# A list schedule for a four-layer graph network on one Trainium2 core: the bound on small matmuls applied in every state, and separate offsets for the second group of a pair

## The chip, the cores and the metric

The kernel runs on one core of one Trainium2 chip. The metric is the device time of one execution in microseconds (us). Before the change it is 2170.12 us, the median of three runs (2168.34 to 2181.28).

## The reference

128 graphs of 64 nodes with 512 features each go through four layers; everything is fp32. After each layer `x = layernorm(x + layer(x))`.

```python
# layer 0: attention from one vector; y = x @ w, s = y @ a
A = exp(leaky(tanh((s_i + s_j) / 8) * 8)) * adj;  A = A / rowsum(A) * rowsum(adj)
out = A @ x @ w
# layer 1: weight = adj * exp((x Wq^T)(x Wk^T)^T), normalised over rows, times x Wv^T
# layer 2: w_i = <q_i, (adj @ (k * mask))_i> * mask / sqrt(512);  out = softmax(w) * (x @ Wv)
# layer 3: two hypergraph convolutions with H = (adj != 0)
h = layer_norm(relu(D^-1 H B^-1 H^T (x @ W1^T) + b1)) * gamma + beta      # 512 -> 1024
out = D^-1 H B^-1 H^T (h @ W2^T) + b2 + x                                 # 1024 -> 512
```

## The kernel before, in words

**Tiling.** Tokens are cut into 64 tiles of 128 (two graphs each). A group is two tiles (256 tokens), so there are 32 groups; a pair is two groups, so there are 16 pairs. One group's work is cut into 16 steps: attention of layer 0 (steps 0 to 2), layer 1 (3 to 6), layer 2 (7 to 11), layer 3 (12 to 15). Steps 0 to 12 are recorded for each group by `run(g)`. Steps 12 to 15 of layer 3 are recorded by `run_rest(n)` for both groups of a pair together, except in the first and the last pair (`APART_3A`), where each group goes alone; there its first product has 512 output columns.

**Two kinds of matmul.** The dense products use the whole 128x128 array ("whole"); they are written as fast matrix products (seven products for eight blocks, forty-nine for sixty-four), with weights streamed from DRAM through eight `ring` buffers. The products with a graph's 64x64 matrices use quarters of the array (mode "quarters": 64 rows, 64 columns, four at a time) and the layer's scores use halves (mode "columns"); both are "divided". `gathered` makes two divided operations of 16 matmuls, so 32 for each 512-feature side; `scores` makes two operations of 8. For the 1024-feature side of layer 3, step 14 of one group needs two `gathered`, that is 64 divided matmuls, and a pair needs 128. `over_graph` has mode "any": one matmul of 128 rows when it is put among whole ones, two of 64 rows when it is put among divided ones. Every fp32 matmul is two passes in the trace, each with its weight load; a transpose is one.

**The order.** The kernel records all operations first, each with an engine, a cost estimate, what it reads and writes, and a key. `Order.run` is a list scheduler: on each engine the ready operation with the smallest key goes next, if its buffers are free. The result is only an order for each engine: the chip executes it in that order and waits on semaphores, and a pause that the scheduler reckoned with is not in the program. The key is `BASE[g]` plus a place in the 16 steps (from how much work still follows the operation) minus an offset: `order.early`, taken from `EARLY[step]`. `PREPARED` places the preparation of weights in the first pairs.

**The choice on TensorE.** All ready TensorE operations go to `Order.choose`. A switch between whole and divided is reckoned with `TURN` 145. While the mode is "whole", a divided operation is taken if it is due earlier than the whole one by more than `NEAR` (by more than 0 where 48 divided matmuls are ready). While the mode is divided, another divided operation is taken only if it is due no later than `FAR` behind the first whole one, and if the last 64 matmuls that end with it take at least 3500 (`BLOCK, REST = 64, 3500`, in ns of the scheduler's reckoning):

```python
        if first[0][0] < 0 or first[0][2].mode == "any" or not (whole and divided):
            return first
        if mode == "whole":
            ...
        fits = [f for f in divided if f[0][0] <= whole[0][0][0] + self.FAR
                and now + f[0][2].cost >= began[f[0][2].matmuls - self.BLOCK] + self.REST]
```

So this bound holds in one state only: the mode is divided and a whole operation is ready as well. With no whole operation ready, with the first operation of negative key, or on the way from whole to divided, it is not asked.

**Buffers.** Eight PSUM banks (`bank`), eight `ring` buffers for weights, 14 of `k4`, two of `h`. `product` is a count, not memory: so many dense products may be under way at once, each with two banks for its running sums and more for single products.

All instructions that the scheduler orders carry line 1459 in the profile (the call in `pinned`), so they are told apart by the names of their tiles: `kept,h` is the gather of step 14, `kept,x` that of step 12, `e,x` that of step 1, `k,k` the scores, `k,e` the attention times values, `e,same` the `over_graph`, `bh,kept` and `ones,adj` the preparation of a chunk of adjacency; `ring,k`, `ring,h` and `k,m` are the dense products, `ident,x` the transposes.

## Time and profile before

| what | value |
|---|---|
| median of three runs | 2170.12 us |
| the profiled execution | 2169.41 us |
| its span (first to last instruction) | 2167.3 us |
| granted TensorE clock, mean | 0.993 |
| TensorE matmul busy | 2118.1 us, 98% of the span |
| VectorE, ScalarE, GpSimd busy | 1489.6, 1205.9, 455.2 us |
| passes on TensorE | 21467 |
| DMA | 422.36 MB, 195 GB/s mean |
| distance from one pair to the next, mid-kernel | 132.0 us |

The profiled execution is 0.7 us under the median, and its span 2.1 us under its own time. The profile page gives busy time by engine, the span in 40 slices, and the costliest groups; the answers to "what did this engine wait for" and the timeline name an idle stretch and what ended it. "issue" as the thing waited for means that no semaphore, DMA or engine in the profile ended the wait. A pass's shown duration is longer than the distance to the next pass, because passes overlap; what a pass costs is read from the distance between starts.

### The profile page before, as it was taken

To read this page: it belongs to the slowest core of one execution; us is meant where nothing else is said; L and a number is where in the kernel's file an instruction comes from. 1 tells how busy PE (TensorE), PEld (TensorE's weight loads), DVE (VectorE), ACT (ScalarE), POOL (GpSimd) and SP (SyncE) were. 2 spreads that over 40 slices of the span, in tenths; PEclk is the share of its full clock that TensorE was granted. 3 is DMA by queue.
4 is the path that set the end of the run, shared out by engine and by line. 5 is a ranking of instruction groups with operands and counts; after the bars stand their busy time and mean duration, and the time that the engine had idled before them with its cause. 6 is when DMAs were issued, how large, how long until landed. Compare 5 with 4: busy or idle time off the path is not lost.

```text
span 2167.3 us, 54072 instructions
## 1 busy us (share of the span) xinstructions
PE 2118.1 (98%) x21467; PEld 1839.7 (85%) x21467; DVE 1489.6 (69%) x4346; ACT 1205.9 (56%) x2698; POOL 455.2 (21%) x434
## 2 busy tenths in 40 slices
PE   8999999999999999999999999999999999999998
PEld 4898788888888888888888888888888988888885
DVE  5766776685766858667686676867667686675854
ACT  2554855564555646466464565645556456564645
POOL 1210421212212112121221202122121121202211
PEclk9999999999999999999999999999999999999999
DMA  8887875554646546465563655536464464545545
GB/s 283 279 279 270 308 245 185 193 186 150 218 140 210 180 168 206 135 203 177 183 220 110 212 183 188 193 127 226 145 215 165 162 216 145 192 159 189 185 171 193
DMA packets 166315, 422.36 MB, mean 195 GB/s; under 512 B 34928, under 2 KB 52528, under 8 KB 166064
## 3 DMA queue, kind: packets, MB, share of 16 engines
q1 hardware_dynamic: 166064, 418.92, 56.3%
q8 instruction: 169, 2.77, 0.5%
q14 instruction: 82, 0.67, 0.1%
HBM read 382.77 MB, written 36.08 MB: 193 GB/s over the span
## 4 chain that ended last, share of the span: by engine, by line
PE 95%; issue 1%; DMA 1%; DVE 1%; ACT 1%; SPq 0%; POOLq 0%; DVEq 0%; ACTq 0%
PE bank L1459 95%; ACT k L1459 1%; DVE k L1459 1%; DMA k<-in_wk_dram 0%; DMA adj<-mask_rows 0%; SPq L1459 0%; DMA ring<-w 0%; DMA adj<-in_adjT_dram 0%; DVE h L1459 0%; ACT e L1459 0%; ACT h L1459 0%; DVE x L1459 0%; DVE col L1459 0%; DVE ring L1459 0%; ACT m L1459 0%
## 5 line engine op out<-in xcount | busy, mean ns | idle before, releaser
L1459 PE MATMUL bank<-ring,k 128*128 128x256 f32 x4940 | 1178.3, 388 | 5.7 <-ACT k L1459 4.1
L1459 PEld LDWEIGHTS bank<-ring,k 128*128 128x128 f32 x4940 | 909.0, 191 | 154.4 <-issue 23.5
L1459 ACT COPY k<-bank 128x512 f32<-128x512 f32 (+1 forms) x934 | 429.2, 484 | 485.0 <-PE bank L1459 378.6
L1459 DVE SCALAR_TENSOR_TENSOR x<-bank,col,x 128x256 f32<-128x256 f32 (+1 forms) x832 | 402.1, 502 | 242.8 <-PE bank L1459 231.4
L1459 PEld LDWEIGHTS bank<-k,m 128*128 128x128 f32 x3584 | 434.2, 192 | 13.3 <-DVE col L1459 1.3
L1459 PE MATMUL bank<-k,m 128*128 128x128 f32 x3584 | 441.4, 276 | 0.3 <-DVE col L1459 0.3
L1459 DVE TENSOR_TENSOR k<-bank,k 128x256 f32<-128x256 f32 (+1 forms) x678 | 296.7, 459 | 182.5 <-PE bank L1459 140.1
L1459 POOL TENSOR_TENSOR col<-col,mhalf 128x2 f32<-128x2 f32 (+1 forms) x161 | 111.1, 693 | 880.4 <-DVE col L1459 509.4
L1459 ACT ACTIVATE k<-x,col 128x512 f32<-128x512 f32 x256 | 184.2, 722 | 189.9 <-DVE col L1459 188.9
L1459 PE MATMUL bank<-ring,h 128*128 128x256 f32 x1024 | 233.1, 381 | 0.0
L1459 ACT ACTIVATE x<-x,col,col 128x512 f32<-128x512 f32 x256 | 199.9, 812 | 59.3 <-DVE col L1459 59.2
L1459 PEld LDWEIGHTS bank<-ring,h 128*128 128x128 f32 x1024 | 193.2, 190 | 27.0 <-issue 1.5
L1459 DVE TENSOR_TENSOR k<-k 128x256 f32<-128x256 f32 (+1 forms) x349 | 145.5, 432 | 47.0 <-ACT k L1459 45.8
L1459 DVE TENSOR_TENSOR k<-k,k 128x256 f32<-128x256 f32 (+3 forms) x361 | 176.6, 493 | 0.5
L1459 POOL TENSOR_TENSOR k<-k,b3b_b 128x512 f32<-128x512 f32 x64 | 80.7, 1272 | 320.6 <-DVE k L1459 289.9
L1459 POOL TENSOR_TENSOR x<-x,bv_b 128x512 f32<-128x512 f32 x64 | 81.3, 1274 | 272.9 <-PE bank L1459 233.0
L1459 PEld LDWEIGHTS bank<-k,k 128*64 128x64 f32 (+1 forms) x2112 | 77.5, 140 | 38.6 <-issue 20.1
L1459 PE MATMUL bank<-k,k 128*64 128x64 f32 (+1 forms) x2112 | 104.8, 238 | 5.3 <-DMA k<-in_wk_dram 4.8
L1459 PEld LDWEIGHTS bank<-kept,h 64*64 64x64 f32 x4096 | 72.7, 140 | 37.9 <-issue 34.0
L1459 ACT ACTIVATE k<-bank,u_c 128x128 f32<-128x128 f32 x256 | 81.8, 364 | 41.2 <-PE bank L1459 34.3
L1459 PE MATMUL bank<-kept,h 64*64 64x64 f32 x4096 | 78.4, 226 | 24.8 <-issue 24.8
L1459 DVE TENSOR_SCALAR col<-col 128x2 f32<-128x2 f32 (+2 forms) x402 | 72.6, 190 | 40.1 <-ACT k L1459 33.9
(102 smaller groups left out, 1677.9 us busy)
## 6 DMA issues: line engine op xcount, KB each, us to landing
ring<-3a SPq DMA_DIRECT2D x196, 512.0 KB, 4.8
ring<-v SPq DMA_DIRECT2D x189, 512.0 KB, 4.2
ring<-3b SPq DMA_DIRECT2D x126, 512.0 KB, 4.8
ring<-w SPq DMA_DIRECT2D x93, 512.0 KB, 4.2
x<-in_x_dram SPq DMA_DIRECT2D x32, 512.0 KB, 6.2
ring<-v SPq DMA_DIRECT2D x63, 256.0 KB, 4.9
out_dram<-x SPq DMA_DIRECT2D x31, 512.0 KB, 6.7
ring<-w SPq DMA_DIRECT2D x31, 256.0 KB, 3.8
```

The lines of the kernel that those rows point to most:

```text
L1459: made = f(*args, **kwargs)
```

## The change

Four edits.

1. In `choose` the 3500 bound filters the divided operations at the top, so in every state. If divided operations are ready, none is allowed and no whole or "any" operation is ready, `choose` returns nothing and the scheduler asks again 100 ns later (in its own reckoning; the order of the program holds no pause).
2. `product` goes from 2 to 3.
3. The second group's and the first group's parts of steps 13 and 14 get different offsets: `LEAD`, times the number of groups that follow in the pair, so the first group of a pair gets 0.325 and -0.58 on top, the second nothing.
4. The numbers `BASE`, `PREPARED`, `FAR` and two entries of `EARLY` are set anew. The distance between pairs in `BASE` stays 8.3 (4.5 + 3.8 before, 4.6 + 3.7 after).

No operation is added to or taken from the recorded list; only the order changes, and with it how many `over_graph` are one whole or two divided matmuls.

```diff
-PREPARED = [-1.85, 7.399, 8.218, 15.311, 12.896, -0.62]
+LEAD = [0.325, -0.58]
+PREPARED = [-5.214, 7.399, 8.218, 12.615, 11.711, -0.62]
...
-    NEAR, FAR = 0.5, 4.0
+    NEAR = 0.5
+    FAR = 5.712
     ENOUGH = 48
 
-    EARLY = [2.22, 0.44, 0.0, 0.0, 0.0, -0.394, 0.0, 1.328, 0.0, 0.57, -0.17, -0.03, -0.766, -0.36, -1.408, -0.35]
+    EARLY = [2.22, 0.626, 0.0, 0.0, 0.0, -0.394, 0.0, 1.328, 0.0, 0.456, -0.17, -0.03, -0.766, -0.36, -1.408, -0.964]
...
         divided = sorted(found.get("quarters", []) + found.get("columns", []), key=lambda f: f[0][:2])
+        allowed = [f for f in divided if now + f[0][2].cost >= began[f[0][2].matmuls - self.BLOCK] + self.REST]
+        if divided and not allowed and not (whole or either):
+            return None
+        divided = allowed
         first = min((f[0] for f in (whole, divided, either) if f), key=lambda f: f[0][:2])
...
-        fits = [f for f in divided if f[0][0] <= whole[0][0][0] + self.FAR
-                and now + f[0][2].cost >= began[f[0][2].matmuls - self.BLOCK] + self.REST]
+        fits = [f for f in divided if f[0][0] <= whole[0][0][0] + self.FAR]
...
-                        found, takes = self.choose(found_pe, mode, now, began)
-                        skipped.remove(found)
+                        chosen = self.choose(found_pe, mode, now, began)
+                        if chosen is None:
+                            n += 1
+                            heappush(events, (now + 100, n, None, None))
+                        else:
+                            found, takes = chosen
+                            skipped.remove(found)
...
-    kinds["product"] = [None] * 2
+    kinds["product"] = [None] * 3
...
         for r, (g, xt, _, in_g, own, dc, dh) in enumerate(pair):
             step(13)
+            order.early += LEAD[0] * (n - 1 - r)
...
             step(14)
+            order.early += LEAD[1] * (n - 1 - r)
```

## The prediction, made before the changed kernel ran

> **What bounds the kernel now.** I read the page first (busy time, the 40 slices), then what TensorE waited for, then the timeline of one such wait, then the granted clock there.

> ```profile
> PE 2118.1 (98%) x21467; PEld 1839.7 (85%) x21467; DVE 1489.6 (69%) x4346; ACT 1205.9 (56%) x2698; POOL 455.2 (21%) x434
> ...
> q8 instruction: 169, 2.77, 0.5%
> ```

> TensorE is the bound; VectorE and ScalarE have a third and more of the span free. The queue named "instruction" moved 169 packets of 16 KB. Matmuls and weight loads are 2 x 21467 = 42934 instructions, 254 for each packet: this queue carries TensorE's own program, about 64 matmuls of two passes for each packet.

> ```profile
> PE bank L1459 <- issue: 25.9, 14, 2.8
> PE bank L1459 <- DMA k<-in_wk_dram: 4.8, 2, 4.2
> PE bank L1459 <- ACT e L1459: 4.5, 3, 3.7
> PE bank L1459 <- ACT k L1459: 4.1, 5, 1.6
> ```

> Columns: waited for; us in total, times, longest. Over half of TensorE's waiting was for nothing that the profile shows. The timeline of the worst one (start, us, instruction):

> ```profile
> 604.98 1.15 PE L1459 MATMUL bank<-k,k 128*64 128x64 f32 x32
> 606.06 1.63 PE L1459 MATMUL bank<-kept,h 64*64 64x64 f32 x96
> 607.62 0.38 PE L1459 MATMUL bank<-row_of,e 128*128 128x2 f32 x2
> 607.93 1.09 PE L1459 MATMUL bank<-k,e 64*64 64x512 f32 x8
> 608.84 0.87 PE L1459 MATMUL bank<-kept,h 64*64 64x64 f32 x44
> 612.54 1.46 PE L1459 MATMUL bank<-kept,h 64*64 64x64 f32 x51 [2.82 <-issue]
> ```

> Before the gap 182 passes, nearly all divided, ran in 4.7 us: 364 instructions, more than a packet. An instruction packet began to move 0.3 us after the gap opened and took 1.07 us; the passes went on 1.4 us after it had landed. TensorE had run out of program. The waits return every 132 us from 347 to 1667, once a pair, eleven times, always in the divided matmuls of step 14. They also slow what follows:

> ```profile
> core 0: us, PE busy (x) PEld busy (x) DVE busy (x) ACT busy (x) POOL busy (x), PEclk, DMA share, GB/s
> 345.00:357.00 12.00, 9.77 (x249) 8.91 (x249) 7.82 (x22) 7.91 (x20) 0.69 (x1) 0.86 0.35 132
> 480.00:492.00 12.00, 10.72 (x162) 9.57 (x153) 9.06 (x29) 8.85 (x23) 1.38 (x2) 1.00 0.13 42
> 609.00:621.00 12.00, 9.09 (x219) 8.34 (x208) 6.64 (x19) 8.02 (x22) 0.61 (x1) 0.86 0.11 42
> 1005.00:1017.00 12.00, 9.79 (x212) 8.92 (x205) 7.30 (x22) 7.78 (x22) 0.98 (x2) 0.86 0.07 26
> ```

> PEclk 0.86 over 12 us is 3.4 us at half clock; five of the eleven stretches have it.

> [...]

> **The price of a stall.** Take the spacing from each pass to the next in the trace, by kind: 216 ns behind a whole pass of 256 columns, 112 behind one of 128, 429 of 512, 109 behind a transpose, 15 to 16 between quarter passes, 30 between score passes. Summed over the order of all 21467 passes that is 2089 us; from the first to the last start the trace has 2155.4. So 66 us are waiting: in the eleven stretches 4.1, 1.8, 4.9, 1.5, 2.9, 4.1, 3.7, 4.1, 1.7, 3.7 and 4.9, in all 37.4; in the first 65 us 10.9; in the last 50 us 1.9; the rest in crumbs of under 0.5. The stalls cost 37.4, not 25.9, because of the slower passes behind them (in the one shown, 4.9 against a gap of 2.82).

> **The change, part by part.** It shows in the compiled order, which I compared.

> *Bound in every state: -37.4 us.* Divided runs without a whole matmul between them were up to 114 matmuls, nine of them of 102; now nearly all have 56 at most, and the one of 118 mixes gathers with the slower scores (its quickest 128 passes take 3.0 us). What counts is a block: the quickest 128 successive passes in the spacings above. Before: 1.9 us in nine pairs and 2.0 to 2.2 in three more places that are over 150 passes wide; eleven of these twelve stalled. Places of 3.1 to 4.3 us, ten of them, show no gap over 0.5 us; three narrow ones of 2.23 us (17 to 86 passes) near the end show no issue wait. After: 4.07 us in nine pairs, 3.0, 3.3 and 3.5 at three other places, and 2.23 (17 wide) once at the end. All that stalled is gone, all that is left is like what did not stall. In the stretch of step 14 the order now has 48 `kept,h`, then 8 whole matmuls (16 x 216 = 3.5 us), then 48, and so on. Bounds: a gain of 37.4 if no fetch is late, of about 25 if every pair keeps 1 us; nothing if the packet needs over 4 us.

> *More switches: +3 to +6 us.* 250 switches instead of 230. Into divided a pass costs 309 instead of 216 ns, out of it 149 instead of 15: 227 ns for a round trip, x 10 = 2.3 us. Twenty `over_graph` become whole: 2 x 112 instead of 4 x about 38 ns, 20 x 0.07 = 1.4 us; together 3.7. The spacings summed over the whole new order (21427 passes) give 2095.8, that is +6.4, with 43 neighbours that the trace lacks priced by the nearest kind. I take 5.

> *Third product, offsets, BASE: 0, from -3 to +8.* They add no instruction. What could go wrong is a wait on a bank, on evacuation, or on weights. A `ring` buffer's time from its last reader (or the load ahead of it in SP's queue, where later) to the first use of its new weights, along TensorE's spacings, was 3.1 us at worst in every middle pair before and is 4.8 after; loads land in 4.2 to 4.8 us and TensorE waited 0.3 us for them in all. So cover grows in the middle. In the first 330 us, where the queues are fullest (275 GB/s, DMA share 0.79), fifteen loads have 4.4 to 8 us, thirteen before. The work that hides evacuation is the whole products between divided runs; each uncovered one costs a ScalarE copy, 0.48 us. VectorE and ScalarE do the same list, and stand at 69% and 56%.

> *Start and end: +2.* The first 132 matmuls keep their order, so the 3.7 us wait for `ACT e` at 47 us stays, with its spell of half clock. At the end the second group's gather now stands among the first group's last products, which hides a wait of 0.9 us, but the first group's gather comes straight behind the wide product without the 1.6 us pause and the 32 `kept,x` that went ahead of it, so the copy behind it is uncovered: 0.6 before, about 2.5 after.

> Sum, from the profiled execution: 2169.4 - 37.4 + 5 + 2 = 2139.0. The median was 0.7 above that execution: 2139.7, rounded to 2140.

> **Rivals.**

> 1. *The fetch stays late.* The bound counts matmuls over a time, the packet comes when it comes. If a packet takes 4.5 us from request to use, each of the nine windows of 4.07 us and the three narrower ones still stall by about 0.5 to 1.5 us, and some bring half clock on top: +10 to +15, so 2150 to 2155. For it: the packet in the shown gap began to move only after the gap opened. Against it: ten places of 3.1 to 4.3 us without a gap.
> 2. *The first pairs lose.* Weight preparation is moved (`PREPARED`), so in SP's queue reloads of layer 0 and 2 weights now stand ahead of and among its stores; if three or four of the fifteen tight loads land 2 to 3 us late, +8 to +10: 2148 to 2150.
> 3. *Slower: a bank wait in every pair.* Three products under way hold six of eight banks; gathers need two, transposes one. If a divided run then waits for a bank at its start, TensorE stands still for copy and handoff, about 0.6 us (0.48 and the semaphore). The gain is 37.4 - 7 = 30 us, 1.9 for each of 16 pairs; so from three or four such waits in every pair there is no gain, and slower by 1% (52 us lost, 3.2 a pair) takes five to six. Against it: waits for `ACT k` were 4.1 us in the whole kernel before, five in number, and the scheduler starts an operation only when its banks are free.
> 4. *It does nothing.* Excluded: the runs of 102 are gone from the program.

> **How the numbers follow.** Forecast 0.74, own range 2133 to 2147; rival 1 0.13 (2147 to 2156); rival 2 0.08; rival 3 0.05 (over 2165). One per cent of the median, about what a measurement can tell from no change, puts the line at 2148.4. Faster by over 1%: the forecast and a little under half of rivals 1 and 2, 0.82. Within 1%: the rest of these two and a part of rival 3, 0.14. Slower: 0.04. The range for 8 in 10 leaves out rival 3, the worst of rival 1 and the best tail of the forecast (no crumbs left, no cost of switches): 2132 to 2156.

> **What would show it.** Right: issue waits of TensorE from 25.9 to under 3 us; no window of half clock between 60 and 2100 us and a mean clock of 0.995 or more; 128 to 130 us from pair to pair instead of 132; 21427 passes. Wrong in the first part: issue gaps in the stretches with `kept,h`, about one at each run. Wrong in the third: rows of TensorE waiting for `ACT k`, `DVE k` or `DMA ring` of over 10 us in all, and in which window they lie tells rival 2 (under 350 us) from rival 3 (each pair).

## The result and the profile after

The changed kernel takes 2160.87 us, the median of seven runs (2158.28 to 2165.27), against 2170.12 (2162.81 to 2181.28, seven runs) for the kernel before: ratio 0.9955, 95% interval 0.9931 to 0.9979. It is faster by half a per cent, which is less than the one per cent that the prediction took as its line, and 21 us over the forecast. The profiled execution took 2158.28 us, its span is 2156.5 us (before 2169.41 and 2167.3), its mean clock 0.997 (before 0.993).

The page after, engine row and instruction queue:

```profile
PE 2118.2 (98%) x21427; PEld 1833.8 (85%) x21427; DVE 1480.0 (69%) x4346; ACT 1195.4 (55%) x2698; POOL 457.5 (21%) x434
...
q8 instruction: 169, 2.77, 0.5%
```

The order is the forecast one (21427 passes), the same 169 packets on the instruction queue (16.4 KB each), and TensorE's busy time has not changed. What TensorE waited for, after (us in total, times, longest):

```profile
PE bank L1471 <- issue: 12.8, 9, 3.7
PE bank L1471 <- DMA k<-in_wk_dram: 5.1, 1, 5.1
PE bank L1471 <- ACT k L1471: 4.9, 5, 1.9
PE bank L1471 <- ACT e L1471: 4.5, 3, 3.7
```

The waits for nothing shown were halved, from 25.9 to 12.8, where the prediction wanted under 3. The rows below it are within 0.8 us of where they were; `ACT k`, which rival 3 would have raised in every pair, is one of them. The longest of the nine is longer than any before. Its timeline (start, us, instruction):

```profile
341.94 1.63 PE L1471 MATMUL bank<-kept,h 64*64 64x64 f32 x96
...
345.10 0.57 PE L1471 MATMUL bank<-kept,h 64*64 64x64 f32 x23
349.37 0.50 PE L1471 MATMUL bank<-kept,h 64*64 64x64 f32 x9 [3.70 <-issue]
349.64 1.93 PE L1471 MATMUL bank<-e,x 64*64 64x64 f32 x64
```

This is the mixed place of which the prediction said that its quickest 128 passes take 3.0 us. The 64 passes after the gap took 1.93 us; the trace has 64 such passes in about 1.1 us at full clock. The windows around it:

```profile
core 0: us, PE busy (x) PEld busy (x) DVE busy (x) ACT busy (x) POOL busy (x), PEclk, DMA share, GB/s
345.00:347.00 2.00, 0.67 (x29) 0.47 (x26) 1.20 (x5) 1.39 (x6) 0.00 (x0) 1.00 0.98 384
...
350.00:353.00 3.00, 3.00 (x69) 1.71 (x62) 0.69 (x1) 2.05 (x4) 0.00 (x0) 0.58 0.49 167
```

The reader is to see two things: the granted clock goes down at the end of the gap (0.58 in this window; the clock's records have 0.50 for 3.41 us, from 349.10), and while TensorE stands still the DMA engines are busy (share 0.98, 384 GB/s).

**The same sum as in the prediction, after.** The nominal spacings over the order give 2095.8 us, from the first to the last start the trace has 2143.94, so 48.1 us are waiting (66.0 before): 17.7 booked for the stretches, where 37.4 was before; 8.9 in the first 65 us (10.9); 3.9 at the end (1.9); 17.6 in crumbs and small waits (15.8). The split depends on the spacings assumed. Mean spacings by tile and shape, taken from the trace of the kernel before, give about 36 us in the eleven stretches before and 15 in them after, and 4 more near 1926 and 2061 us, where two of the nine gaps stand and the kernel before had none: 19 in all. From pair to pair it is 129.8 us in the middle (1261.8 to 1521.4 is two pairs), forecast 128 to 130, before 132.0.

### The profile page after: what moved, and what is told of

Its sections match the earlier page's. It is cut to its first block, busy times and chain, and to the rows that moved or that the text cites. A ratio compares the mean times of both kernels' runs of the same rounds, so it can differ in the third digit from the quotient of the medians.

```text
span 2156.5 us, 53957 instructions
## 1 busy us (share of the span) xinstructions
PE 2118.2 (98%) x21427; PEld 1833.8 (85%) x21427; DVE 1480.0 (69%) x4346; ACT 1195.4 (55%) x2698; POOL 457.5 (21%) x434
## 3 DMA queue, kind: packets, MB, share of 16 engines
q1 hardware_dynamic: 166064, 418.92, 57.5%
q8 instruction: 169, 2.77, 0.5%
## 4 chain that ended last, share of the span: by engine, by line
PE 95%; DMA 2%; ACT 1%; issue 1%; DVE 1%; SPq 0%; POOLq 0%; DVEq 0%; ACTq 0%
PE bank L1471 95%; DMA ring<-v 1%; ACT k L1471 1%; DMA adj<-mask_rows 1%; DVE k L1471 0%; ACT h L1471 0%; SPq L1471 0%; DMA ring<-3a 0%; DMA k<-in_wk_dram 0%; DVE x L1471 0%; DVE col L1471 0%; ACT e L1471 0%; ACT x L1471 0%; DVE ring L1471 0%; ACT m L1471 0%
## 5 line engine op out<-in xcount | busy, mean ns | idle before, releaser
L1471 PE MATMUL bank<-ring,k 128*128 128x256 f32 (+1 forms) x4940 | 1185.8, 388 | 7.9 <-ACT k L1471 4.8
L1471 DVE TENSOR_TENSOR k<-k 128x256 f32<-128x256 f32 (+1 forms) x349 | 151.6, 454 | 47.0 <-ACT k L1471 44.2
L1471 POOL TENSOR_TENSOR k<-k,k 128x1024 f32<-128x1024 f32 (+1 forms) x31 | 72.0, 2323 | 141.8 <-DVE k L1471 107.7
L1471 DVE TENSOR_TENSOR h<-k,k 128x1024 f32<-128x1024 f32 (+1 forms) x88 | 89.9, 1025 | 16.8 <-POOL k L1471 8.2
L1471 DVE TENSOR_SCALAR col<-col 128x2 f32<-128x2 f32 (+2 forms) x402 | 78.7, 199 | 24.4 <-ACT k L1471 18.0
```

Of the source, the lines that this page charges most:

```text
L1471: made = f(*args, **kwargs)
```

## Where the packets fall

Where divided passes go on right behind a stall in the kernel before (boundaries at 874.8, 1273.2 and 1535.6, DMA share 0.08 or less), packets begin to move 1.1 to 1.2 us after the boundary, and with the 0.95 us that a packet takes and the 1.4 us until the passes go on, they would go on about 1.2 + 0.95 + 1.4 = 3.55 us after it. This is an estimate, and it counts from the boundary, because the trace doesn't show when a packet is asked for (where the expectations say "request", read the boundary). A low share alone doesn't make the packet early: behind the gap at 615.95 it began 3.2 us after its boundary under a DMA share of 0.01, where whole passes came next; these 256 instructions lasted 5.6 us, and no gap followed. So only like places are compared below. At the gaps after the change the packets began later:

| boundary, us | next packet begins | DMA share until then | gap, us |
|---|---|---|---|
| 342.4 | 4.67 us later | 0.84 | 3.90 |
| 478.4 | 2.92 | 1.03 | 1.68 |
| 611.0 | 2.77 | 0.88 | 1.04 |
| 871.0 | 2.78 | 0.96 | 1.18 |
| 1130.7 | 2.10 | 1.09 | 0.57 |
| 1261.8 | 2.77 | 0.83 | 1.23 |
| 1521.4 | 2.94 | 0.99 | 1.39 |
| 1920.8 | 3.52 | 0.96 | 1.89 |
| 2055.3 | 3.29 | 0.86 | 1.72 |

The gap is counted here from start to start of the passes around it, less their usual spacing; the profile's figure is 0.2 us less. The share is the last column but one of these windows of the kernel after, each from a boundary to the start of the packet; it sums the times of all packets, and where they overlap it can pass 1:

```profile
478.40:481.30 2.90, 2.90 (x105) 2.02 (x99) 2.07 (x11) 1.97 (x7) 0.56 (x1) 1.00 1.03 330
...
871.00:873.80 2.80, 2.80 (x78) 2.24 (x75) 2.10 (x7) 2.80 (x4) 0.18 (x1) 1.00 0.96 366
...
1521.40:1524.30 2.90, 2.90 (x78) 2.20 (x74) 1.23 (x5) 2.90 (x5) 0.00 (x0) 1.00 0.99 315
```

For 342.4 the sum is 4.67 + 0.92 + 1.4 = 7.0 us, and the passes go on at 349.37; the 4.4 us of two expectations below is an estimate of mine between this and 3.55. In the gap that the prediction showed (boundary 606.4, packet 3.62 later) the DMA share was 1.03 from 606 to 608 and 0.93 to 610. So the theory to test, A, a guess from these windows: weight loads under way hold the packet back; from its boundary the passes go on 3.55 us later where the DMA share is low and up to 7 later where it is high, and a pair stalls where a boundary falls in its divided stretch and loads are under way. Theory B (the forecast's): what counts is only how densely divided matmuls stand, and the remainder has a fixed cause, another wait or a packet that always takes over 4 us. Rival C: the gain that is there comes from the bound itself; against it, under A, most of it comes from the new numbers.

## Experiments

Three batches; the kernel before had a median of 2169.69, 2171.14 and 2169.57 us in them, and ratios are against it on the same chip.

**1 and 2. The order unchanged, less on the DMA engines.** The streamed loads are cut to 128 columns, so products use zeros or old weights for the rest; one execution each. With the order after, the queue of loads and stores has 18.5% of the DMA engines' time instead of 57.5.

```diff
+    for t_ in kinds["ring"]:
+        nc.gpsimd.memset(t_, 0.0)
...
-                      lambda t_=t_, src=src, n=n, width=width: nc.sync.dma_start(
-                          out=t_.t[:, : n * width], in_=src.t[:, : n * width]),
+                      lambda t_=t_, src=src: nc.sync.dma_start(out=t_.t[:, :128], in_=src.t[:, :128]),
```

> The kernel before, with every streamed weight load cut to 128 of its up to 1024 columns (the ring buffers are zeroed at the start, so products use zeros or old weights for the rest); order on each engine unchanged. Theory A [...]: a packet follows its request in about 3.5 us when the engines are free, so gaps of TensorE on issue shrink from 25.9 us to 8 to 16, packets start within 1.2 us of a boundary where dispatch is not ahead, and the time falls by 10 to 20 us. Rival B (fetch takes as long whatever the DMA does, or another limit in TensorE's front end): gaps stay at 22 to 28 us.

> The same cut of the weight loads in the changed kernel. Theory A: the remaining 12.8 us of issue gaps vanish (under 2 us), time 2138 to 2150. Rival B: 10 to 15 us of issue gaps stay.

Measured: 2142.76 us with the order of before, 2135.81 with the order after. Waits of TensorE in the first:

```profile
PE bank L1460 <- issue: 7.9, 7, 1.7
```

and the first row of the second, where there is none for issue:

```profile
PE bank L1472 <- DMA k<-in_wk_dram: 6.0, 2, 4.2
```

The place of the worst gap, in the timeline of the second:

```profile
339.68 1.63 PE L1472 MATMUL bank<-kept,h 64*64 64x64 f32 x96
...
342.22 0.69 PE L1472 MATMUL bank<-k,k 128*64 128x64 f32 x16
342.83 1.01 PE L1472 MATMUL bank<-kept,h 64*64 64x64 f32 x29
```

The same instructions in the same order run through. Two of the boundaries of the table, those of 611.0 and 1261.8, in this run:

```profile
602.00:604.80 2.80, 2.80 (x70) 2.06 (x66) 2.53 (x12) 2.80 (x4) 0.62 (x1) 1.00 0.11 29
1248.00:1251.00 3.00, 3.00 (x84) 2.26 (x79) 2.68 (x13) 3.00 (x5) 0.61 (x1) 1.00 0.10 27
```

At these two the next packet begins 0.43 and 0.83 us later, at those of 342.4 (DMA share 0.58 from 339 to 342 us, around it), 478.4, 871.0 and 1521.4 it is 0.53, 0.23, 0.37 and 0.73; five of the six gaps are 0.10 us or less, the one of 3.90 is 0.26. The data in the products is no rival cause: the spacings are the same with and without the cut (216 ns behind a whole pass of 256 columns, 15 between quarter passes). Here A holds and B falls: with the loads cut the changed order shows no issue wait, which is what was forecast of it. With the order of before, the cut took away 18 of the 25.9 us of issue waits; the rest, 7.9, stays without it: divided runs of 102 matmuls are too quick there too. In that run the passes go on 3.0 to 3.9 us after the boundary, all seven gaps stand where a packet's 256 instructions last 1.9 to 2.8 us, and those that last 3.0 us or more have no such gap over 0.21 us. Both times fell by more than the issue waits (27 and 25 us against 18 and 12.8); what holds the rest was not shown.

**3, 4. The bound alone, and all but the bound.** Kernel before with edit 1; kernel after without it.

```diff
+        allowed = [f for f in divided if now + f[0][2].cost >= began[f[0][2].matmuls - self.BLOCK] + self.REST]
+        if divided and not allowed and not (whole or either):
+            return None
+        divided = allowed
```

> The kernel before with the first edit alone: bound in every state, old numbers, two products. In its order the quickest 128 passes of each pair are 2.2 us against 1.9 before and 4.1 after, because the scheduler meets the bound with pauses of its own that the program does not hold; 252 switches. Theory A: gaps fall only a little, to 17 to 24 us, and the time is 2158 to 2170, so that most of the gain comes from the new numbers. Rival C (the bound itself is what helps): 2155 to 2162, gaps under 15 us.

> The changed kernel without the first edit: old choice, new numbers, three products and the offsets of the first group. Its order has windows of 3.8 to 4.1 us in most pairs, but four of 2.2 and one of 1.9; 266 switches, nominal spacings 2097.4 us. Theory A: issue gaps 12 to 20 us, time 2160 to 2172. Rival C (the bound itself is what helps): no gain over before, gaps above 22 us.

Measured: the bound alone 2182.14 us, ratio 1.0044 (1.0029 to 1.0059), slower by 0.4%, against both forecasts. All but the bound 2163.48, ratio 0.9973 (0.9962 to 0.9983). Waits with the bound alone, and in the last row with all but the bound:

```profile
PE bank L1467 <- issue: 15.0, 9, 2.2
PE bank L1467 <- ACT k L1467: 7.9, 9, 2.5
...
PE bank L1467 <- DVE x L1467: 2.7, 3, 1.3
...
PE bank L1463 <- issue: 12.3, 8, 3.2
```

The bound alone does take issue waits away (25.9 to 15.0), but the scheduler often has no whole operation ready to put between and meets the bound with a pause that the program doesn't hold (the quickest 128 passes of its order are still 2.2 us in a pair), and new waits on ScalarE and VectorE come in. The other three edits alone leave 12.3 us of issue waits, no more than the 12.8 with the bound on top, and have most of the gain. So rival C falls: neither the gain nor the fall of the issue waits needs the bound. What the bound adds, 0.9973 to 0.9955, is not shown, because the intervals overlap.

**5. The same order, other boundaries.** 32 matmuls of one column ahead of the kernel after move every boundary by half a packet.

```diff
+    for _ in range(32):
+        tc.nc.tensor.matmul(kinds["bank"][7][:64, :1], same[:, :64], ones, start=True, stop=True)
```

> The changed kernel with 32 small matmuls of one column (128 instructions, half a packet) on TensorE ahead of its first work, in time in which it waits for its first load; every order is otherwise the same, so that packets are cut at other places of the program. Theory A: gaps come only where a packet's 256 instructions take under about 4.4 us, so they move: those near 615, 875, 1267 and 1527 us vanish, new ones of 0.3 to 1.5 us come near 745 and 1396 us, the ones near 350 and 485 stay (there the cut falls badly either way), and one or two may come near 1787. Gaps 6 to 11 us in all, time 2154 to 2162. Rival D (the gaps belong to places in the work, such as a busy DMA or a bank, not to the cut of the program): gaps at the same places, 12 to 14 us.

Measured: 2167.58 us, ratio 0.9985 (0.9973 to 0.9997). They cost about 4 us at the start (the first product of the order begins at 8.74 instead of 5.11 us), more than I had reckoned. The issue waits are 14.1 us in twelve gaps, over the 6 to 11 of the forecast. So neither time nor total speaks for A; the places do. Kernel after, one of its nine gaps:

```profile
873.98 1.09 PE L1471 MATMUL bank<-kept,h 64*64 64x64 f32 x59
876.04 0.80 PE L1471 MATMUL bank<-kept,h 64*64 64x64 f32 x37 [0.98 <-issue]
```

The shifted kernel in a pair where the kernel after has no gap:

```profile
1661.63 0.99 PE L1471 MATMUL bank<-kept,h 64*64 64x64 f32 x53
1665.33 0.91 PE L1471 MATMUL bank<-kept,h 64*64 64x64 f32 x43 [2.71 <-issue]
```

The gaps near 615, 876, 1267 and 1527 are gone, as forecast; new ones stand at 750, 1401 and 1799 us, near places that were forecast, and at 1662, which was not; all twelve again at 192 or 193 of 256. At 1662 the packet began 4.2 us after its boundary. The same order stalls in other pairs when only the packet boundaries move; what the loads of that moment add is not shown here.

**6, 7. Fewer loads under way.** Each streamed load of the kernel after waits until the second (or third) load before it has landed.

```diff
+        loads.append(made.ins.name)
+        if len(loads) > UNDER:
+            tc.add_manual_dep(made.ins, loads[-1 - UNDER], ...)
```

> The changed kernel, with each streamed weight load made to wait on SP until the second load before it has landed, so that two are under way at most instead of eight. Order on TensorE unchanged. Theory A: [...] issue gaps fall from 12.8 to under 6 us; waits for ring loads may rise from 1.5 to 5 to 20 us, above all in the first 330 us, so the time is 2150 to 2168. Rival B (fetch is slow whatever is in the DMA queues): gaps stay at 11 us or more.

> The same with three loads under way at most. Theory A: gaps 5 to 10 us, ring waits under 6 us, time 2150 to 2160. Rival B: gaps 11 us or more.

Measured: two under way 2181.45, ratio 1.0055 (1.0039 to 1.007); three 2157.62, ratio 0.9941 (0.9926 to 0.9957), which can't be told from the kernel after. Waits with two, and in the last row with three:

```profile
PE bank L1480 <- DVE col L1480: 9.8, 9, 1.8
PE bank L1480 <- DMA ring<-v: 6.1, 6, 2.6
...
PE bank L1480 <- issue: 2.7, 5, 1.4
...
PE bank L1480 <- issue: 11.1, 9, 2.6
```

With two the issue waits went from 12.8 to 2.7, as A wants, and more came back elsewhere. The chain of waits between 1268 and 1280 us shows one case (start, us, what):

```profile
1270.13 4.66 DMA adj<-mask_rows
...
1274.89 0.43 DVE kept L1480
```

Before these rows the chain shows 3.89 us of a `ring` load; the small transfer of mask rows was issued only after it had landed, VectorE stood for that, and TensorE behind VectorE until 1277 us.

With three the issue waits are 11.1, a miss: A had 5 to 10, and 11 or more was the mark of B. The packets show why. At the nine boundaries of the table, counted by instruction, eight packets still begin 2.0 to 3.8 us later with three loads. With two, five of the nine begin at most 1.5 us later, though the DMA engines can be as busy: the boundary of 478.4, now at 482.6, has 1.4 us under a share of 0.96, where it had 2.92 under 1.03. The other four begin 2.1 to 3.8 us later. So the busy share alone doesn't set the delay. With two loads under way four of the nine packets begin 2.0 us late or more, with three eight; what in the loads delays a packet was not shown.

**8, 11. A higher bound.** REST of 5500 and of 4300 in the kernel after.

> The changed kernel with 5500 instead of 3500 in the bound, nothing else. 310 switches instead of 250; spacings of the undisturbed trace summed over its order give 2103.5 against 2095.8 us. The quickest 128 passes are 4.6 us or more in most places. Theory A: issue gaps under 5 us, so 12.8 - 4 gained and 7.7 paid: 2155 to 2163. Rival E (3500 is enough, gaps have another cause): gaps stay near 12 and the time rises by the 7.7, to 2166 to 2172.

> The changed kernel with 4300 instead of 3500 in the bound, nothing else. 296 switches, undisturbed spacings 2100.0, the quickest 128 passes 4.4 to 4.7 us in the middle pairs, a few places of 2.1 to 3.3 at the ends. Theory A (a packet needs about 4.4 us when weight loads keep the DMA engines busy): issue gaps 3 to 7 us, so 6 to 10 gained, 4 paid, if no new waits for weights come: 2152 to 2160. Rival H (as with 5500 a tighter bound costs more in waits for weights and evacuation than it saves): 2162 to 2172.

Measured: 2175.69, ratio 1.0029 (1.0013 to 1.0044), and 2165.29, ratio 0.997 (0.9956 to 0.9984). With 5500 the issue waits are nearly gone:

```profile
PE bank L1471 <- DMA ring<-w: 9.4, 5, 2.1
PE bank L1471 <- ACT k L1471: 6.8, 10, 2.3
...
PE bank L1471 <- issue: 0.3, 1, 0.3
```

and it buys nothing: 310 switches instead of 250 put the nominal spacings at 2103.5 (+7.7), and TensorE waits 9.4 us for `ring<-w` and 6.8 for `ACT k`, where the kernel after has none of the first and 4.9 of the second. The profiled execution, 2167.14 us, is the fastest of its seven, so what the median lost beyond it is not in these rows. With 4300 the issue waits are 3.3 us, the nominal spacings 2100.0, `ACT k` 8.1 and `ACT e` 6.7. In these two runs a higher bound takes from the issue waits and pays at least as much in switches and other waits: 4300 can't be told from 3500 (the intervals overlap), and 5500 is slower.

**9, 10, 12. Third product and offsets.** In the kernel after `product` back to two; in the kernel after LEAD at 0, 0; in the kernel before edit 1 with the third product.

```diff
-    kinds["product"] = [None] * 3
+    kinds["product"] = [None] * 2
```

```diff
-LEAD = [0.325, -0.58]
+LEAD = [0.0, 0.0]
```

> The changed kernel with two products under way instead of three; bound, offsets and numbers as in the change. Order: 282 switches, undisturbed spacings 2095.4 us (as the change: 2095.8), the quickest 128 passes 3.7 us in nine pairs and 2.1 to 2.2 at four places. Theory A: issue gaps 14 to 20 us against 12.8, so 2160 to 2170. Rival F (the third product costs bank waits and is where the gain is lost): waits for ACT k and DVE x fall, time under 2156.

> The changed kernel with the offsets of the first group of a pair set to 0. Order: 282 switches, undisturbed spacings 2098.4, 128 passes in 3.9 to 4.1 us at two places of each pair instead of one. Theory A: gaps 12 to 20 us, time 2161 to 2170. Rival G (the offsets cost time): under 2157.

> The kernel before with the bound in every state and three products, old numbers, no offsets of the first group. Order: 258 switches, spacings 2096.5, 128 passes in 2.2 us in nearly every pair. Theory A: gaps 14 to 22 us as with the bound alone, time 2165 to 2185. Rival C (the bound with room for a third product is what helps): 2155 to 2162, gaps under 13 us.

Measured: two products 2171.54, ratio 1.001 (1.0 to 1.002); no offsets 2175.55, ratio 1.0027 (1.0015 to 1.004); the bound and the third product on the kernel before 2189.75, ratio 1.0093 (1.0072 to 1.0114). Waits of the first of these:

```profile
PE bank L1471 <- issue: 7.4, 7, 2.2
PE bank L1471 <- ACT k L1471: 6.6, 7, 1.9
```

Here my expectation missed: issue waits did not rise, they fell to 7.4, and the 11 us were lost to many small waits for copies and loads (61.4 us of waiting in all against 48.1). Without the offsets the issue waits are 12.2, as in the kernel after, so its loss lies in other waits too (`ACT k` 8.6). Nor does the third product carry the gain: with the bound, on the old offsets, the kernel is slower still and its issue waits are 16.3, so a third product alone doesn't give the bound the whole operations that it lacked. It looks as if the planner's numbers, the third product, the offsets and the bound were fitted to each other: taking away any one of the last three costs 4 to 16 us by the ratios, of which the 4 of the bound is within the noise. No version that I ran is clearly faster than the kernel after.

Over all twelve, the forecasts of theory A had the issue waits within their range in seven, and the time in two. Eight of the other times were longer than forecast: the issue waits were foreseen better than what the rest of the order does when one rule is changed.

## Why the prediction was wrong, point by point

**The bound: forecast -37.4, measured -19.7** (about -17 with the second set of spacings). This term was mis-sized, and the step that failed is the sentence "All that stalled is gone, all that is left is like what did not stall". It took ten places of 3.1 to 4.3 us per 128 passes without a gap as proof that such a place doesn't stall. The runs showed what counts besides, a boundary and a load. In the kernel before, three packets whose 256 instructions last 3.8 to 4.0 us (boundaries at 1804.5, 1926.9 and 2055.2) had the next one begin 1.0 to 1.2 us later, under a DMA share of 0.06, 0.11 and 0.53, and no gap; after the change packets that last as long (1261.8 and 1521.4) had it begin 2.8 and 2.9 us later under 0.83 and 0.99, and stalled. I had one sign of this in hand, a packet that began to move after the gap had opened, and put it into a rival of 0.13. The windows that the prediction shows took in the time after the gap and so have low DMA shares (0.07 to 0.35); the two stretches of 2 us up to the gap at 610 us, read afterwards, have 1.03 and 0.93. Rival 1 had the late packet, with a time of 4.5 us and 10 to 15 us left; from the boundary to the next pass it was 4.9 to 7.0 us at the nine gaps, and 17.7 us are left.

The term also had the wrong owner. The prediction compared the whole new order with the old one and booked the wider spacing of the divided runs under the first edit. Experiments 3 and 4 show that the first edit alone leaves 15.0 us of issue waits and makes the kernel slower, while the other three alone leave 12.3.

**More switches: forecast +5 from +3 to +6.4; +6.4 taken.** This is the sum over the compiled order again, not a measurement of its own. What speaks for it is that the trace after has the same prices: 309 ns into divided passes, 148 to 149 out of them, 216 behind a whole pass.

**Third product, offsets, BASE: forecast 0, left over +1.8** in crumbs and small waits for `ring`; the border between this and the first term is uncertain by some 3 us. The weights hold in the first pairs (rival 2 has one wait there, 0.7 us for `ring`), and no bank wait appears in each pair (rival 3: `ACT k` 4.1 to 4.9). But 0 was right only for the four edits together; experiments 3, 9, 10 and 12 show that edits which add no instruction move 4 to 20 us between them.

**Start and end: forecast +2, measured +0.6**: first load 0.9 later, first 65 us 2.0 better, end 2.0 worse as worked out, after the last pass 0.3 better.

Sum: -19.7 + 6.4 + 1.8 + 0.6 = -10.9; the spans differ by 10.8 (2167.3 - 2156.5), which the terms must add up to, as the crumbs take what is left over. The forecast had -30.4.

**Signs named in advance.** Passes and the distance of pairs came as said, the mean clock too (0.997); issue waits (12.8, not under 3) and the window of half clock at 350 us came out against the first part, and no sign of the third did.

## What to carry to other kernels

Where an engine waits for nothing that the profile shows, count its instructions. Here all 23 such gaps of the two kernels stood at 192 or 193 of 256, and behind each an instruction packet had landed 1.2 to 1.5 us before the passes went on. What a gap cost went with two times from the boundary: how long the 256 instructions last (3.1 to 4.3 us at the nine gaps after) and when the passes can go on (4.9 to 7.0 us there, under a DMA share of 0.83 to 1.09). A quiet place that did not stall proved nothing for a busy one: 3.8 to 4.0 us at a share of 0.06 to 0.53 had no gap, the same time at 0.83 and 0.99 had one. And this order, fitted as a whole, answered to one rule changed in it by waits elsewhere, so a gain of a rule is to be forecast together with what the scheduler will do instead.

## What the runs showed of the hardware

With the streamed loads cut TensorE goes on 3.0 to 3.9 us after a boundary (the seven gaps of the order before); at the gap of 349.37 after the change, with a DMA share of 0.98 and 384 GB/s ahead of it, it took 7.0 us. The difference lies before the packet begins to move (0.2 to 0.8 us in the changed order with the loads cut, 2.8 to 4.7 at the same six boundaries with them), while its own 0.9 to 1.5 us are the same in both. What holds the packet back in that time is not shown; the runs with two and three loads under way show only that it begins at most 1.5 us late at five of the nine boundaries with two, and 2.0 to 3.8 us late at eight with three.

The length of a gap alone doesn't decide on half clock, a granted clock of 0.50 in the records. The gap of 3.7 us (the profile's figure, as all in this paragraph) came with a clock of 0.58 over the 3 us from 350.00, and the eight shorter issue gaps after the change, up to 1.7 us, were followed by a clock of 1.00. But in the kernel before five gaps of 2.0 to 2.8 us were followed by 3.4 us of half clock, and two of 2.1 and 2.4 us (ending at 1535.6 and 1273.2) were not; and a wait of 1.9 us for `ACT k`, ending at 2119.5 after the change, was.
